# When the zeros of four accumulators are written, and by whose queue: a graph layer with scatters

## The chip, the cores and the metric

The kernel runs on one core of a Trainium2 chip. The metric is the device time of one execution in microseconds (us), median of several runs; less is better. The core has five engines that run side by side, each with its own instruction stream in order: PE (matrix products; PEld is its weight load), DVE and ACT (element work), POOL (here above all the indexed scatters) and SP (here only issues DMAs). DMAs can be issued from SP, ACT and POOL.

## The reference, cut to what matters

```
h = relu(layernorm(x))                              # 6250 nodes x 128
x1 = h @ W_in
W_ij = (ssp(f_ij @ W_f1 + b_f1) @ W_f2 + b_f2) * cutoff    # 200000 edges
out = segment_sum(x1[dst] * W_ij, src, 6250)
return x + ssp(out @ W_o1 + b_o1) @ W_o2 + b_o2     # ssp(v) = softplus(v) - log 2
```

Here dst, by which x1 is gathered, is sorted; src, by which the sum is made, is random.

## The kernel before, in words

**Quads.** The edges are cut into 391 quads of 512 edges. A software pipeline (line 944) takes one quad an iteration: in iteration i, z of quad i+1 (feature matmul, `s1_pe`), softplus of quad i (`s1_exp`, `s1_ln` on ACT, `s1_guard` on DVE), gather and second matmul of quad i-1 (`s2_pe_x`, `s2_pe_w`), their product (`s2_m`), the sum of equal rows of quad i-2 inside chunks of 128 edges (`s3_pe`), its copy for quad i-3 (`s3_copy`, line 377, ACT) and the scatter of quad i-4 (`s3_scatter`). A copy goes to a staging tile `s`, of which there are five: the copy of a quad waits until the scatters of the quad five plain quads before it have landed.

**Plain and sorted quads.** From quad 8 on, two of five quads are "sorted": they are permuted by node group and added in SBUF (`accT`), and only their overflow is scattered. Quads 0 to 7 are all plain, with four scatters each; then 9, 11, 12, 14, 16 and so on are.

**Scatters.** A scatter adds 128 rows to one of four accumulators in memory (`acc0` to `acc3`, 6400 rows of 128 floats). It is an indirect DMA with addition issued by POOL, and it waits until the previous scatter into the same accumulator has landed. `acc_of` gives scatter k its accumulator: 0 below `K1_END` = 2, k % 2 below `K2_END` = 8, k % 3 below 140, then k % 4.

**Zeros.** Each accumulator must be zero before its first scatter. `zero_piece` writes a tenth, 320 KB, from a zeroed tile. POOL issues accumulator 0's ten pieces. SP issues accumulator 1's ahead of the loop (line 773), behind the loads of quads 0 to 3 (`load_sc(0)`, `load_sc(1)`) and a feature block (`fb_load(1)`). Lists `Z2` and `Z3` tell at which iteration SP issues each piece of accumulators 2 and 3: 0, 0, 1, 1, 2, 2, 3, 3, 4, 4 and 5, 7, ..., 23. Within an iteration such a hook comes after the loads of that iteration.

**Loads.** `load_sc(s)` loads features (`ft`), source indices (`sb`), relative rows (`rb`) and table rows (`wn`) of quads 2s and 2s+1, and is called at iteration 2s-4; its tiles have three buffers. `half_load(k)`, at iterations 1 and 2, loads the index rows of the second half of the edges, which DVE turns into relative rows in `half_piece` (line 723) two or more iterations later.

**Order.** The order of instructions on each engine follows the order of the calls (`manual_schedule`). In the built program each DMA issued from SP or ACT takes one of eight completion counters in turn, and waits before it is issued until the DMA eight places earlier, from either engine, has landed.

Of the kernel before, what the change touches and what calls it, by code (L numbers as in the profile page):

```python
# [46 lines left out]
def tile_gnn(ctx: ExitStack, tc: tile.TileContext, x, fB, cT, srcT, srcr, dstr, win_, wf1, wf2, bias, bo1c, wo1,  # L47
             wo2, consts, ident, out, n_edges):
    nc = tc.nc
# [17 lines left out]
    ACC_R = NP + P  # L67
    GN = NP // GRP
    ZR = 10 if ACC_R % 10 == 0 else 1
    K1_END, K2_END, K3_END = 2, 8, 140  # L70
    Z2, Z3 = [0,0,1,1,2,2,3,3,4,4], [5+2*j for j in range(10)]
    CE = min(128, EP // P)
    mpq = sorted_quads(NQ)
    mpi = {q: n for n, q in enumerate(mpq)}
# [68 lines left out]
    def zero_piece(eng, k, j, parts=1):  # L143
        v = accs[k].rearrange("(p t) f -> p (t f)", p=P).rearrange("p (r e) -> r p e", r=ZR)
        w = ACC_R // ZR // parts
        for h in range(parts):
            eng.dma_start(v[j][:, h * w:(h + 1) * w], zero[:, :w])
# [66 lines left out]
    def prep_rm(g):  # L214
        T = groups[g][1]
        rm = wk.tile([P, 4, P], F32, tag="rm", name="rm", bufs=1)
        nc.vector.tensor_tensor(rm[:, :T], pst[g]["xs"][:, :T], pst[g]["x3"][:, :T, 0], op=ALU.subtract)
        pst[g]["rm"] = rm

    def prep_x2(g):  # L220
        T = groups[g][1]
        nc.scalar.copy(pst[g]["x3"][:, :T, 1], pst[g]["rm"][:, :T])

    def prep_x3(g):
        o, T = groups[g]
        w = T * P
        x3 = pst[g]["x3"]
        nc.vector.tensor_tensor(x3[:, :T, 2], pst[g]["rm"][:, :T], x3[:, :T, 1], op=ALU.subtract)
        tab_write(g)

    def tab_write(g):
        o, T = groups[g]
        nc.sync.dma_start(tab[o * 3:(o + T * P) * 3, :].rearrange("(t p k) f -> p t k f", t=T, k=3),
                          pst[g]["x3"][:, :T])
        del pst[g]

    def fb_load(b):
        t_ = ld.tile([P, FE], F32, tag="fb", name="fb", bufs=2)
        nc.sync.dma_start(t_, fB[b].rearrange("r e -> (r e)").rearrange("(p e) -> p e", p=P))
        fst[b] = {"f": t_}  # L240
# [424 lines left out]
    def src_cast(s, lo, hi, eng, tag, **kw):  # L665
        s16 = wk.tile([HALF, hi - lo], I16, tag=tag, name="s16", **kw)
        eng.tensor_copy(s16, idx[s, lo][1])
        nc.sync.dma_start(src16[s * HALF:(s + 1) * HALF, lo:hi], s16)

    with tc.manual_schedule():  # L670
# [77 lines left out]
        prep_x1(0)  # L748
        prep_rm(0)
        prep_x2(0)  # L750
        prep_x3(0)
        src_cast(0, 0, SC, nc.gpsimd, "pt")
        ws = cp.tile([K1, P], BF16, name="ws")
# [16 lines left out]
            load_sc(1)  # L770
        if NB > 1:
            fb_load(1)
        for j in range(ZR):
            zero_piece(nc.sync, 1, j)

        hooks = {}

        def at(i, point, fn, *a):
# [524 lines left out]
```

## Time and profile before

| | us |
|---|---|
| runs of the kernel before: median (lowest to highest) | 2117.85 (2117.82 to 2121.36) |
| the profiled execution | 2119.3 |
| its span | 2117.0 |
| POOL busy in the span, x1073 | 1695.6 |
| PE, DVE, ACT busy | 1915.6, 1763.7, 1789.3 |

The page shares busy time by engine, cuts the span into 40 slices of 53 us, and follows the chain that ended last. Its first slices differ from the later ones:

```
PE   3778999999999999998989999999999999998946
DMA  7987767777777777777777777777777777777639
GB/s 265 242 183 132 149 129 146 141 157 144 149 141 147 133 151 145 141 145 142 148 133 157 139 136 152 143 146 152 136 146 139 129 152 137 139 154 144 111 38 241
```

A digit is the busy share of a slice in tenths. In the first three slices PE is not yet full and the DMA engines move more than later. The other views used below are the timeline (start, length, engine, line, operation, and in brackets the engine's idle time before it with what ended it), the chain of waits (start, length, what), and windows (length, busy time of PE, PEld, DVE, ACT and POOL with counts, granted clock of PE, DMA share, GB/s).

### The profile page before, as it was taken

Reading aid. Unit: us, or ns where it says so; the run is one execution under the profiler, and the core shown is the slowest. Engines: PE = TensorE matmul, PEld = TensorE weight load, DVE = VectorE, ACT = ScalarE, POOL = GpSimd, SP = SyncE. Lnnn points to the kernel's source line nnn. Section 1 sums busy time; section 2 is a strip of 40 time slices with the busy share of each in tenths; the row PEclk is TensorE's granted clock in tenths of the full one; section 3 lists DMA queues with packets and bytes.
Section 4 is the critical chain, followed back from the end, with each engine's and each line's share of the span. In section 5 each row is a group of like instructions: output and inputs, shape, how many; then the busy total and the mean of one; then the engine's idle time right before and its main releaser. Section 6 shows DMA issues by size and latency. Waiting matters only on the chain.

```text
span 2117.0 us, 56533 instructions
## 1 busy us (share of the span) xinstructions
PE 1915.6 (90%) x19769; PEld 1392.3 (66%) x19769; DVE 1763.7 (83%) x4710; ACT 1789.3 (85%) x4781; POOL 1695.6 (80%) x1073
## 2 busy tenths in 40 slices
PE   3778999999999999998989999999999999998946
PEld 2556667676666667666767677777767666766724
DVE  4768888888989898888898989889888878897825
ACT  4688889998988899898989999999899898988804
POOL 2678888888888888888888888888888888887874
PEclk9899999999999999999999999999999999999977
DMA  7987767777777777777777777777777777777639
GB/s 265 242 183 132 149 129 146 141 157 144 149 141 147 133 151 145 141 145 142 148 133 157 139 136 152 143 146 152 136 146 139 129 152 137 139 154 144 111 38 241
DMA packets 395696, 315.17 MB, mean 149 GB/s; under 512 B 94959, under 2 KB 335130, under 8 KB 395410
## 3 DMA queue, kind: packets, MB, share of 16 engines
q1 hardware_dynamic: 245858, 240.57, 38.9%
q0 software_dynamic: 149264, 70.91, 35.3%
q8 instruction: 155, 2.54, 0.5%
q14 instruction: 131, 1.07, 0.2%
q10 hardware_dynamic: 288, 0.07, 0.0%
HBM read 173.32 MB, written 138.06 MB: 147 GB/s over the span
## 4 chain that ended last, share of the span: by engine, by line
PE 32%; ACT 20%; DVE 19%; DMA 10%; POOL 10%; issue 7%; SPq 2%; ACTq 0%; DVEq 0%; POOLq 0%
POOL acc L417 10%; DMA acc<-s,ji 8%; PE un L620 8%; PE W L347 7%; PE pq L527 6%; ACT xc L352 5%; PE pp L369 4%; ACT mst L533 3%; DVE so L605 3%; ACT e L295 3%; ACT e L294 2%; ACT e L300 2%; DVE pm L503 2%; ACT s L377 2%; DVE a L324 1%
## 5 line engine op out<-in xcount | busy, mean ns | idle before, releaser
L417 POOL DMA_INDIRECT acc<-s,ji x955 | 1538.3, 1611 | 350.3 <-issue 222.8
L527 PE MATMUL pq<-pt,pm 128*128 128x387 bf16 x2432 | 484.1, 339 | 26.5 <-ACT s L377 19.2
L352 ACT ACTIVATE xc<-xg,cb 128x128 f32<-128x128 f32 x1564 | 446.4, 374 | 46.9 <-PE xg L339 45.0
L347 PE MATMUL W<-w,a 128*128 128x128 f32 x3128 | 461.7, 292 | 0.0
L347 PEld LDWEIGHTS W<-w,a 128*128 128x128 f32 x3128 | 386.2, 194 | 41.8 <-issue 2.3
L620 PE MATMUL un<-so,mst 32*128 32x392 bf16 x7296 | 355.1, 331 | 41.8 <-DVE pr L467 18.4
L527 PEld LDWEIGHTS <-pm 128*128 128x128 bf16 x2432 | 238.6, 99 | 187.7 <-issue 36.1
L620 PEld LDWEIGHTS <-mst 32*128 32x128 bf16 x7296 | 223.0, 94 | 169.3 <-issue 63.0
L324 DVE SCALAR_TENSOR_TENSOR a<-z,e 128x512 f32<-128x512 f32 x391 | 267.2, 683 | 70.2 <-ACT e L300 70.0
L300 ACT ACTIVATE e<-e,con 128x512 f32<-128x512 f32 x391 | 282.3, 722 | 12.7
L369 PEld LDWEIGHTS pp<-m,eq 128*128 128x128 f32 x1912 | 255.0, 195 | 37.2 <-DVE accT L631 23.6
L369 PE MATMUL pp<-m,eq 128*128 128x129 f32 x1912 | 261.4, 280 | 17.0 <-DVE accT L631 15.0
L533 ACT CAST mst<-pq 128x387 bf16<-128x387 f32 x608 | 260.4, 480 | 8.3 <-PE pq L527 8.3
L377 ACT COPY s<-pp 128x258 f32<-128x258 f32 x478 | 167.1, 391 | 116.2 <-PE pp L369 64.8
L295 ACT ACTIVATE e<-e 128x512 f32<-128x512 f32 x391 | 246.5, 630 | 12.4
L294 ACT ACTIVATE e<-z 128x512 f32<-128x512 f32 x391 | 242.0, 619 | 16.7 <-PE z L289 16.1
L357 DVE TENSOR_TENSOR m<-W,xc 128x512 f32<-128x512 f32 x239 | 164.0, 686 | 80.4 <-ACT xc L352 75.4
L517 DVE TENSOR_TENSOR pt<-pt 128x512 f32<-128x512 f32 x304 | 209.9, 691 | 0.0
L503 DVE TENSOR_SCALAR pm<-iot,pos 128x576 bf16<-128x576 f16 x608 | 197.5, 387 | 0.0
L631 DVE TENSOR_TENSOR accT<-un,accT 128x392 f32<-128x392 f32 x288 | 142.5, 556 | 47.3 <-PE un L620 32.1
L357 DVE TENSOR_TENSOR pt<-W,xc 128x512 f32<-128x512 f32 x152 | 104.5, 688 | 82.1 <-ACT xc L352 80.7
L289 PE MATMUL z<-ft,ws 123*128 123x512 bf16 x391 | 151.9, 389 | 17.9 <-DMA ft<-fsd 17.9
(156 smaller groups left out, 2693.2 us busy)
## 6 DMA issues: line engine op xcount, KB each, us to landing
sb<-src SPq DMA_DIRECT2D x195, 256.0 KB
ft<-fsd SPq DMA_DIRECT2D x195, 240.0 KB
rb<-reld SPq DMA_DIRECT2D x391, 64.0 KB
fsd<-f SPq DMA_DIRECT2D x49, 480.0 KB
fb<-in_fB_dram SPq DMA_DIRECT2D x49, 320.0 KB
fsd<-f SPq DMA_DIRECT2D x49, 320.0 KB
acc<-s,ji POOLq DMA_INDIRECT x955
wn<-tab SPq DMA_DIRECT2D x782, 15.8 KB
```

The source lines that it names most:

```text
L294: nc.scalar.activation(e, st[q]["z"], AF.Abs)
L295: nc.scalar.activation(e, e, AF.Exp, scale=-1.0)
L300: nc.scalar.activation(e, e, AF.Ln, bias=half, scale=0.5)
L324: nc.vector.scalar_tensor_tensor(a, st[q]["z"], 0.0, st[q]["l"], op0=ALU.max, op1=ALU.add)
L347: nc.tensor.matmul(W[:, c, :], st[q]["a"][:, c * P:(c + 1) * P], w2, start=False, stop=(c == 3))
L352: nc.scalar.mul(xc[:, c, :], st[q]["xg"][:, c, :], late["c", q // CQ][:, 4 * (q % CQ) + c:4 * (q % CQ) + c + 1])
L357: nc.vector.tensor_tensor(m[:, :, :P], st[q]["W"], st[q]["xc"], op=ALU.mult)
L369: nc.tensor.matmul(pp[:, c, :129], st[q]["eq"][:, k, :], m[:, k, :129], start=True, stop=True)
L417: nc.gpsimd.indirect_dma_start(out=accs[k][:, :], out_offset=bass.IndirectOffsetOnAxis(ap=ji, axis=0), in_=s, in_offset=None, compute_op=A ...
L527: nc.tensor.matmul(t[:, :PW], mp[q]["pm"][:, c, s * P:(s + 1) * P], high(mp[q]["pt"][:, c:c + 1, :PW])[:, 0], start=(c == 0), stop=(c == 3))
L533: nc.scalar.copy(mp[q]["ms", s][:, :PW], mp[q].pop(("q", s))[:, :PW])
L620: nc.tensor.matmul(ts[g][:, :GN], mp[q]["ms", s][v, k * P:(k + 1) * P], mp[q]["oh"][v], start=(q == qs[0] and k == 0), stop=(q == qs[-1] a ...
```

## The change

Accumulator 1's zeros are issued from ACT, after the second part of the table is made (`prep_x2(0)`) and ahead of ACT's first work on a quad. The pieces of accumulator 2 are issued at iterations 2 to 8, those of accumulator 3 at 11 to 20, one in each. Accumulator 2 takes part from scatter 20 on instead of 8.

```diff
-    K1_END, K2_END, K3_END = 2, 8, 140
-    Z2, Z3 = [0,0,1,1,2,2,3,3,4,4], [5+2*j for j in range(10)]
+    K1_END, K2_END, K3_END = 2, 20, 140
+    Z2, Z3 = [2, 3, 4, 5, 6, 6, 7, 7, 8, 8], [11 + j for j in range(10)]
...
         prep_x2(0)
+        for j in range(ZR):
+            zero_piece(nc.scalar, 1, j)
         prep_x3(0)
...
             fb_load(1)
-        for j in range(ZR):
-            zero_piece(nc.sync, 1, j)
-
         hooks = {}
```

In the built program SP's and ACT's own order stays as it was apart from these pieces. Scatters 8 to 19 go to accumulators 0 and 1 in turn; all others go where they went.

## The prediction

> **What bounds it now.** I read the page first. Its chain is shared among all engines, and its costliest row is the scatter:
>
> ```profile
> PE 32%; ACT 20%; DVE 19%; DMA 10%; POOL 10%; issue 7%; SPq 2%; ACTq 0%; DVEq 0%; POOLq 0%
> L417 POOL DMA_INDIRECT acc<-s,ji x955 | 1538.3, 1611 | 350.3 <-issue 222.8
> ```
>
> No single engine is the bound. The change touches only iterations 0 to 23, and scatter k lands in the same accumulator as before from k = 20 on. So the question is how much earlier or later the loop leaves its first 120 us; after that everything is carried along one for one. Windows of 140 us show that: PE is busy 79.0 of the first 135 us and 124 to 135 of each later 140.
>
> Then the timeline of 20 to 60 us, for SP's queue and for who waits on it:
>
> ```profile
> 22.96 0.60 ACT L294 ACTIVATE e<-z 128x512 f32<-128x512 f32 x1 [5.91 <-PE z L289]
> 32.62 7.77 SPq L147 DMA_DIRECT2D acc<-accT  x10
> 40.43 0.75 SPq L270 DMA_DIRECT2D ft<-fsd  x1
> 45.57 0.61 PE L289 MATMUL z<-ft,ws 123*128 123x512 bf16 x1 [6.59 <-DMA ft<-fsd]
> 51.36 0.23 DVE L723 TENSOR_SCALAR base_i<-half,con 98x2 int32<-98x2 int32 x1 [8.83 <-DMA half<-in_dstr_dram]
> ```
>
> SP spends 7.77 us on the ten zero pieces of accumulator 1; the feature load of quads 4 and 5 is queued behind them, and PE idles 6.6 us for it. Next DVE idles 8.8 us for a half-index load that stands behind that load and two pieces of accumulator 2.
>
> Last, the chain of waits from 85 to 125 us and POOL's timeline. In the chain "issue" before ACT L377 is a wait for the scatter issued at 108.02 (scatter 23): the copy of quad 12 reuses the staging tile of quad 5.
>
> ```profile
> 91.06 6.63 DMA acc<-s,ji
> 97.96 6.10 DMA acc<-s,ji
> ...
> 108.55 6.54 issue
> 115.08 0.04 ACTq L377
> 115.12 0.04 issue
> 115.16 0.65 ACT s L377 x2
> ```
>
> ```profile
> 49.23 1.65 POOL L417 DMA_INDIRECT acc<-s,ji  x1 [23.90 <-ACT ji L398]
> 56.30 1.65 POOL L417 DMA_INDIRECT acc<-s,ji  x1 [5.42 <-DMA acc<-s,ji]
> 62.34 1.54 POOL L417 DMA_INDIRECT acc<-s,ji  x1 [4.38 <-DMA acc<-s,ji]
> ...
> 68.05 1.53 POOL L417 DMA_INDIRECT acc<-s,ji  x1 [2.33 <-DMA acc<-s,ji]
> ...
> 72.72 1.62 POOL L417 DMA_INDIRECT acc<-s,ji  x1 [1.30 <-DMA acc<-s,ji]
> ...
> 76.58 1.54 POOL L417 DMA_INDIRECT acc<-s,ji  x1 [0.30 <-issue]
> ...
> 101.65 1.63 POOL L417 DMA_INDIRECT acc<-s,ji  x1 [0.30 <-ACT e L295]
> ```
>
> These are scatters 0, 1, 2, 4, 6, 8 and 20. A scatter costs POOL 1.54 + 0.30 = 1.84 us, but the next one into the same accumulator waits for its landing. So the early loop is two races: loads against PE and DVE up to 60 us, the stream of scatters from there to 115 us. The change helps the first and holds the second back.
>
> **1. Ten pieces move from SP to ACT.** SP loses 7.77 us ahead of the load of quads 4 and 5. ACT gains ten issues after L222 ends at 17.05, and they are not ten times the 0.45 us of its two constant loads: in the built program each DMA of SP or ACT waits for the one eight places before it (which is why SP's pieces went out 0.8 us apart after the third). ACT's seventh piece waits for the first quad's ft (used by PE at 22.34), the ninth for rb (used by DVE at 24.66), the tenth for the seventh piece. With the four pieces already in flight delaying these by about 1 us, and about 3 us for the seventh piece to land, the tenth leaves near 27 (estimate). Behind it waits ACT's first exponential, at 22.96 before: +4.5 us. Part of this is hidden: quad 0 waited for wn until 26.73 anyway, and quad 2 for its own load until 31.5. I take z of quad 2 at 33, +1.5. Bounds: 0 if ACT is free at 23; +4.5 if nothing hides it.
>
> The Trainium skill (DMA: Bandwidth & Descriptors, Issuing engines are not separate DMA queues) speaks against a gain: DMAs of all issuers run on the same 16 engines, and a second issuer only saves issue time. Rows of the windows view (DMA share and GB/s last):
>
> ```profile
> 16.00:18.00 2.00, 0.00 (x0) 0.00 (x0) 1.47 (x5) 0.40 (x1) 0.00 (x0) 1.00 0.32 97
> 18.00:20.00 2.00, 0.00 (x0) 0.00 (x0) 1.82 (x8) 0.00 (x0) 0.00 (x0) 1.00 0.70 210
> 36.00:42.00 6.00, 2.95 (x17) 1.87 (x16) 3.20 (x5) 5.33 (x15) 0.00 (x0) 0.93 1.04 411
> ```
>
> By the rule alone the 3.28 MB of zeros delay the load of quads 4 and 5 as much as before: no gain. By the rows they now start where the engines are 30 to 70% idle (16 to 24 us: about 3 us of idle capacity) and not at 36 to 42, where they are full. I take the rows: ft of quads 4 and 5 is issued near 34 instead of 40.4, and z of quad 4 moves from 45.6 to about 42: **-3 us**, bounds 0 (the rule) and -6 (all of PE's stop). Scatter 0 (49.23) follows quad 4's exponentials, so it also starts 3 us earlier. DVE's half-index work gains more, 5 to 7 us, but scatters, not DVE, come last later.
>
> **2. Pieces of accumulators 2 and 3 later.** Eight pieces leave 46 to 60 us, two stay there. Scatters 0 and 1, which both go to accumulator 0, returned after 7.07 and 6.04 us under them (49.23, 56.30, 62.34). Without them I take 5.5 each: -2.1 us. The pieces reappear at iterations 4 to 8, about eight of them where five stood, so no lower return is assumed there. Accumulator 2 is complete near 85 us, well ahead of scatter 20. Accumulator 3 enters at scatter 140 in both: no cost.
>
> **3. Third accumulator at scatter 20 instead of 8.** Twelve scatters alternate between two. From the rows, 8 to 20 took 101.65 - 76.58 = 25.1 us with three. With two, each pair costs one return: 5.71 and 4.67 in the rows of scatters 2, 4 and 6, in a lighter stretch; 6.6 and 6.1 plus 0.3 in the chain of 91 to 104 us, with three in flight. I take 5.5; bounds 4.67 and 6.9. Five returns and two issues: 5 x 5.5 + 2 x 1.84 = 31.2, **+6.1 us** (bounds +2.0 and +13.1). Scatter 8 itself now waits for scatter 6: 2 to 8 becomes 5.71 + 4.67 + 5.5 = 15.9 instead of 14.2: +1.6.
>
> **Sum.** Scatter 8: -3 - 2.1 + 1.6 = -3.5 us. Scatter 20: -3.5 + 6.1 = +2.6. Scatters 20 to 23 and the landing at 115.0 keep their 13.4 us, so ACT's copy moves from 115.2 to 117.8; three pieces that lay at 138 to 156, where POOL leads again, are gone: about -0.5. Total **+2 us**. The profiled execution took 2119.3 (span 2117.0), so 2121.3 for it; it was 1.4 above the median of the runs, so 2120 for the median.
>
> **Rivals.**
> *The gain stays*: with two scatters in flight they return in about 4.4 us (below 4.67, since fewer transfers compete), pair cost 25.7 for part 3, so +0.6 there and +0.5 for scatter 8, and the load stage gives 5: 2112. For it: the shortest returns of the trace are those with two accumulators. Against: DMA share is 0.86 to 1.08 from 78 to 114 us.
> *The stream decides, on the slow side*: pairs return in 6.4 us as the chain of 91 to 104 us has them, +10.6 in part 3, +2.5 at scatter 8, -5 before: +8, 2126. It decides from a return of about 5.9. For it: exactly these waits are the chain now. Against: with two in flight, and PE held back, fewer loads compete.
> *ACT does not get out ahead*: the pieces wait on the first loads and the first loads on them, ACT is late by the full 4.5 us, quad 4 gains nothing: +5, 2123.
>
> **Numbers.** No change can be told within 0.2%, 4.2 us. Forecast 0.44 (2115 to 2122); gain stays 0.21; stream slow 0.27; ACT blocked 0.08. Faster 0.21, same 0.44, slower 0.35. The forecast's own range is 2115 to 2122; the range asked for takes in both bounds of the return and the start, 2112 to 2129.
>
> **What would show it.** Part 1: ACT's first L294 near 27 with L147 on ACT's queue ahead of it; z of quad 4 near 42, PE's 6.6 us stop gone; DVE's L723 near 45. Part 2: returns of scatters 0 and 1 near 5.5. Part 3: scatters 8 to 19 in pairs 5.5 apart, POOL idle for "DMA acc<-s,ji" between 14 and 130 us up from 18.9; ACT L377 of quad 12 near 118 with a longer idle ahead. I am wrong if pairs return in under 4.7 or over 5.9 us, or if the copies of quads 9 to 12 don't wait for scatters.

## The result, and the profile after

The changed kernel takes 2127.49 us (median of 7 runs, 2122.78 to 2130.72); the kernel before took 2117.82 in the same 7 rounds (2113.17 to 2121.36). The ratio is 1.0047, 95% interval 1.0031 to 1.0063: 9.7 us slower, some 7 to 13. The time lies inside the range of the prediction. The forecast case "no change that can be told" did not come; the nearest rival was the slow stream of scatters at 2126. The profiled execution took 2127.5 (span 2125.2), 8.2 more than the one of before.

The page's costliest group hardly moves, since only the first 24 of 391 iterations differ; the shares of the chain shift by up to 5 points against those before (PE 32%, ACT 20%, POOL 10%), which is not read further here:

```profile
PE 37%; ACT 25%; DVE 16%; DMA 9%; issue 7%; POOL 5%; SPq 1%; ACTq 0%; DVEq 0%; POOLq 0%
L417 POOL DMA_INDIRECT acc<-s,ji x955 | 1536.1, 1608 | 359.8 <-issue 215.9
```

The loss is in the first 125 us. Timeline of ACT, PE, SP and DVE after, 15 to 50 us:

```profile
16.63 17.40 ACTq L147 DMA_DIRECT2D acc<-accT  x10
34.13 0.60 ACT L294 ACTIVATE e<-z 128x512 f32<-128x512 f32 x1 [17.16 <-DMA acc<-accT]
...
26.47 1.01 PE L289 MATMUL z<-ft,ws 123*128 123x512 bf16 x2 [13.45 <-DMA ft<-fsd]
35.01 0.58 PE L339 MATMUL xg<-wn,oh 63*128 63x128 bf16 x4 [6.99 <-DMA wn<-tab]
38.79 0.63 PE L289 MATMUL z<-ft,ws 123*128 123x512 bf16 x1
...
46.20 0.38 PE L289 MATMUL z<-ft,ws 123*128 123x512 bf16 x1
...
34.21 0.34 SPq L270 DMA_DIRECT2D ft<-fsd  x1
...
39.84 0.42 SPq L270 DMA_DIRECT2D ft<-fsd  x1
...
49.90 0.22 DVE L723 TENSOR_SCALAR base_i<-half,con 98x2 int32<-98x2 int32 x1
```

The same places before:

```profile
22.34 1.01 PE L289 MATMUL z<-ft,ws 123*128 123x512 bf16 x2 [9.32 <-DMA ft<-fsd]
25.46 1.26 SPq L270 DMA_DIRECT2D ft<-fsd  x1
26.73 0.80 PE L339 MATMUL xg<-wn,oh 63*128 63x128 bf16 x4 [2.84 <-DMA wn<-tab]
31.50 0.58 PE L289 MATMUL z<-ft,ws 123*128 123x512 bf16 x1 [1.98 <-DMA ft<-fsd]
```

ACT stands at its ten zero pieces from 16.6 to 34.0 us, and its first exponential comes 11.2 us later than before (22.96). PE's stop of 6.6 us ahead of quad 4 is gone, but 8.3 us more now lie ahead of quad 0: 13.45 us for its features instead of 9.32, and 6.99 for its table rows instead of 2.84. Quad 2 is 7.3 us late (38.79 against 31.50), quad 4 0.6 (46.20 against 45.57). SP issues the load of quads 2 and 3 8.8 us later than before (34.21 against 25.46), and so that of quads 4 and 5 at 39.84, hardly earlier than the 40.43 of before.

The windows after (DMA share and GB/s last) show where the zeros went:

```profile
18.00:20.00 2.00, 0.00 (x0) 0.00 (x0) 1.83 (x8) 0.00 (x0) 0.00 (x0) 1.00 1.01 377
24.00:30.00 6.00, 1.54 (x3) 0.24 (x3) 0.00 (x0) 0.00 (x0) 1.26 (x3) 1.00 1.02 403
36.00:42.00 6.00, 5.08 (x23) 4.20 (x24) 4.88 (x7) 4.96 (x11) 0.00 (x0) 1.00 0.65 190
```

The engines are now full at 18 to 20 us (0.70 before) and at 24 to 30 (0.98 before), and have room at 36 to 42 us (1.04 before).

Then the stream of scatters, in POOL's timeline after (scatters 0, 1, 2, 8 and 20):

```profile
51.76 1.65 POOL L417 DMA_INDIRECT acc<-s,ji  x1 [26.50 <-ACT ji L398]
57.88 1.57 POOL L417 DMA_INDIRECT acc<-s,ji  x1 [4.47 <-DMA acc<-s,ji]
61.45 1.54 POOL L417 DMA_INDIRECT acc<-s,ji  x1 [2.00 <-DMA acc<-s,ji]
...
79.09 1.54 POOL L417 DMA_INDIRECT acc<-s,ji  x1 [1.81 <-DMA acc<-s,ji]
...
111.30 1.54 POOL L417 DMA_INDIRECT acc<-s,ji  x1 [0.31 <-ACT e L294]
```

The steps, against 49.23, 62.34, 76.58 and 101.65 before: start +2.5; scatters 0 to 2 take 9.7 us instead of 13.1 (-3.4); 2 to 8 take 17.6 instead of 14.2 (+3.4); 8 to 20 take 32.2 instead of 25.1 (+7.1). Together +9.6, and scatter 20 is at +9.65. Between 14 and 130 us POOL waits 28.8 us for landings of scatters, 18.9 before. The chain of waits after hands this on to ACT:

```profile
17.93 6.48 DMA src<-s
...
75.74 6.91 DMA acc<-s,ji
...
82.91 5.82 DMA acc<-s,ji
...
89.00 6.03 DMA acc<-s,ji
...
95.29 5.21 DMA acc<-s,ji
...
109.26 8.53 DMA acc<-s,ji
...
123.97 0.65 ACT s L377 x2
```

From 75 to 100 us it goes from landing to landing in accumulator 1 (scatters 7, 9, 11 and 13); at 123.97 ACT copies quad 12, 8.8 us later than before (115.16), after idle stops of 4.8, 7.4, 2.0, 5.3 and 3.6 us at its copies of this stretch. By their first product on PE (z), quads 16 to 20 are 8.7 to 8.8 us late, and that stays, with some wandering (4.8 to 12.4 from quad 30 on, 7.5 at the last), to the end.

### The profile page after: what moved, and what is told of

It reads as the page before. It is cut to its first block, busy times and chain, and to the rows that moved or that the text cites. A ratio compares the mean times of both kernels' runs of the same rounds, so it can differ in the third digit from the quotient of the medians.

```text
span 2125.2 us, 56530 instructions
## 1 busy us (share of the span) xinstructions
PE 1914.4 (90%) x19769; PEld 1392.6 (66%) x19769; DVE 1762.2 (83%) x4710; ACT 1787.9 (84%) x4781; POOL 1695.4 (80%) x1073
## 4 chain that ended last, share of the span: by engine, by line
PE 37%; ACT 25%; DVE 16%; DMA 9%; issue 7%; POOL 5%; SPq 1%; ACTq 0%; DVEq 0%; POOLq 0%
PE un L620 11%; PE W L347 8%; DMA acc<-s,ji 7%; PE pq L527 7%; ACT xc L352 6%; POOL acc L417 5%; ACT mst L533 4%; PE pp L369 4%; ACT e L295 4%; ACT e L294 3%; ACT e L300 3%; DVE so L605 3%; ACT s L377 2%; DVE pm L503 2%; PE z L289 1%
## 5 line engine op out<-in xcount | busy, mean ns | idle before, releaser
L295 ACT ACTIVATE e<-e 128x512 f32<-128x512 f32 x391 | 246.5, 630 | 12.4
L339 PE MATMUL xg<-wn,oh 63*128 63x128 bf16 x1564 | 156.4, 221 | 13.2 <-DMA wn<-tab 7.0
```

Of the source, the lines that this page charges most:

```text
L295: nc.scalar.activation(e, e, AF.Exp, scale=-1.0)
```

## The experiments

Theory A: most of the loss is the stretch in which scatters alternate between two accumulators. Theory B: it is ACT's stop at its zeros. All times are medians, compared with runs of the kernel before on the same chip. Two places of each trace carry the reading: scatter 20, and ACT's copy of quad 12. A single trace's total is no guide: in their later parts the profiled executions drift by several us against each other. The ratio is an estimate of its own with its interval; it can differ from the quotient of the two medians by 0.0008.

| | edit | scatters 8 to 20 (us) | copy of quad 12 at | median, before | ratio (95%) |
|---|---|---|---|---|---|
| before | | 25.1 | 115.2 | | |
| changed | all | 32.2 | 124.0 | 2127.5, 2117.8 | 1.0047 (1.0031 to 1.0063) |
| e1 | K2_END = 20 alone | 34.4 | 122.7 | 2125.5, 2118.7 | 1.0039 (1.0023 to 1.0055) |
| e2 | zeros on ACT alone | 27.6 | 117.7 | 2119.8, 2118.7 | 1.0008 (0.9998 to 1.0018) |
| e3 | changed, zeros back on SP | 32.8 | 120.6 | 2121.9, 2118.7 | 1.0022 (1.0011 to 1.0032) |
| e4 | changed, ACT's zeros as one DMA | 30.0 | 121.9 | 2126.6, 2118.7 | 1.0043 (1.0024 to 1.0061) |
| d1 | K2_END = 32 alone | 36.3 | 127.8 | 2129.2, 2117.3 | 1.0054 (1.0038 to 1.0070) |
| n1 | K1_END = 0 | 25.1 | 114.4 | 2117.9, 2117.3 | 1.0005 (0.9996 to 1.0015) |
| n2 | K1_END = 0, K2_END = 12 | 28.8 | 114.6 | 2118.0, 2117.3 | 1.0006 (0.9994 to 1.0018) |
| n3 | n2 with later lists | 33.1 | 115.8 | 2116.1, 2117.3 | 0.9986 (0.9974 to 0.9999) |
| e6 | changed, K1_END = 0 | 36.1 | 119.9 | 2126.6, 2119.1 | 1.0029 (1.0015 to 1.0043) |
| n4 | acc1's zeros at iteration 1 | 28.7 | 113.7 | 2116.5, 2119.1 | 0.9985 (0.9969 to 1.0000) |
| n5 | acc1's zeros on POOL | 29.7 | 117.9 | 2117.3, 2119.1 | 0.9993 (0.9981 to 1.0005) |

**e1, K2_END alone.**

```diff
-    K1_END, K2_END, K3_END = 2, 8, 140
+    K1_END, K2_END, K3_END = 2, 20, 140
```

> Only K2_END goes from 8 to 20; zeros stay where they were. Theory A (the two-accumulator stretch is most of the loss): scatter 0 stays at 49.2 us, scatters 8 to 20 take 31 to 32 us instead of 25.1, ACT's copy of quad 12 moves from 115 to 122 or more, time +6 to +8 us against the kernel before. Theory B (ACT's stop at the zeros is the loss, the stretch is hidden): time within 2 us of before, the copy of quad 12 at 115 to 117.

Theory A. Scatter 0 is at 48.6, scatters 8 to 20 take 34.4 us (more than the 31 to 32 expected), and ACT's copy of quad 12 is 7.5 us later. In its timeline, scatters 8 and 20 and the copy:

```profile
78.72 1.54 POOL L417 DMA_INDIRECT acc<-s,ji  x1 [3.23 <-DMA acc<-s,ji]
...
113.17 1.54 POOL L417 DMA_INDIRECT acc<-s,ji  x1 [0.30 <-ACT e L300]
...
122.68 0.65 ACT L377 COPY s<-pp 128x258 f32<-128x258 f32 x2 [5.11 <-issue]
```

**e2, ACT alone.**

```diff
         prep_x2(0)
+        for j in range(ZR):
+            zero_piece(nc.scalar, 1, j)
...
-        for j in range(ZR):
-            zero_piece(nc.sync, 1, j)
```

> Only accumulator 1's zeros move from SP to ACT. Both theories: ACT stands at its zeros until 33 or 34 us and z of quad 2 is near 39. Theory A: the load of quads 4 and 5 makes up most of it, scatter 0 at 50 to 53 us, scatters 8 to 20 in about 25 us, time +1 to +4 us. Theory B: scatter 0 and all behind it are late by what ACT lost, time +8 to +10 us.

ACT starts at 34.1 as in the changed kernel, quad 2 is 7.3 us late and scatter 0 3.7 us. Scatters 2 to 15 are within 1.1 us of before: the late start is absorbed. A delay comes back later (scatter 20 3.5 us, quad 16 2.5 us), and scatters 8 to 20 take 27.6 us instead of about 25. The time is +1.1 us with an interval that takes in none. Theory B, with +8 to +10 us, falls.

**e3, the changed kernel without ACT's part.**

```diff
-        for j in range(ZR):
-            zero_piece(nc.scalar, 1, j)
...
+        for j in range(ZR):
+            zero_piece(nc.sync, 1, j)
```

> The changed kernel with accumulator 1's zeros back on SP, behind the loads of quads 0 to 3. Theory A: scatter 0 near 48 us, scatters 8 to 20 in about 32 us, time +4 to +7 us against before (that is 3 to 5 less than the changed kernel). Theory B: -2 to +1 us against before.

The median is 3.2 us over before, between the two expectations and nearer to A; the ratio, 1.0022, makes it 4.7, inside A. The new lists of zeros do help: scatters 1 to 4 are 3.2 to 5.0 us earlier than before. Then the stretch costs its 7.7 us (32.8 instead of 25.1), and scatter 20 is 7.2 late. Set against the changed kernel (1.0047), ACT's part seems to cost more here than alone (1.0008): with the stream behind at most landings, less absorbs its late start. The intervals of e3 and the changed kernel just touch, so this is likely, not shown.

**e4, one DMA on ACT.**

```diff
-        for j in range(ZR):
-            zero_piece(nc.scalar, 1, j)
+        nc.scalar.dma_start(accs[1].rearrange("(p t) f -> p (t f)", p=P).rearrange("p (r e) -> p r e", r=ZR),
+                            zero.unsqueeze(1).to_broadcast([P, ZR, ACC_R // ZR]))
```

> The changed kernel with the ten pieces on ACT as one DMA of 3.28 MB, which takes one completion counter instead of ten. If the counters hold ACT (each piece waits for a DMA eight places earlier): ACT's first exponential at 23 to 27 us instead of 34.1; the second table load of quad 0 then waits for the whole DMA, so quad 0's product is near 31; scatter 0 at 46 to 50; time 1 to 5 us less than the changed kernel, still over before because of the stretch. If bandwidth holds ACT (an issue lasts until the engines take its bytes): ACT's first exponential at 30 us or later, and the time of the changed kernel.

Neither clause as written. ACT's issue no longer holds it, but its first exponential comes at 29.7, because PE's first product waits for features until 29.12. Timeline of PE in e4:

```profile
29.12 1.01 PE L289 MATMUL z<-ft,ws 123*128 123x512 bf16 x2 [16.08 <-DMA ft<-fsd]
```

and the chain of waits in e4:

```profile
17.96 9.50 DMA src<-s
```

against before:

```profile
18.01 2.56 DMA src<-s
```

That small write of indices, without which SP can't read them back, took 2.56 us before, 6.48 in the changed kernel with five pieces issued around it, and 9.50 here with all of them in front. Quad 2 is at 39.8, as late as with ten pieces (38.8). So freeing ACT gives nothing back: zeros in flight during the first loads delay the loads themselves. SP's own issues are slower too (the four of quads 0 and 1's table rows take 4.9 us in the changed kernel and 2.9 here, 2.2 before); how much of that comes from the counters that it shares with ACT was not separated.

**d1, the stretch twice as long.** K2_END = 32 in the kernel before.

> The kernel before with K2_END = 32: the two-accumulator stretch is twice as long as with 20. If the stream of scatters sets the early loop: scatters 8 to 32 take about 24 x 2.7 = 65 us, some 14 more than before at scatter 32, and the time is +12 to +16 us against before, twice that of K2_END = 20. If the loss of K2_END = 20 was a one-off (one collision of a scatter with loads): +6 to +8 as with 20.

The median is 11.9 us over before, just under what was expected. But the trace tells it otherwise than expected: scatter 20 is 14.1 us late and scatter 32 13.7, so the second half of the stretch lost nothing more against before. There fewer scatters come (from quad 8 on only three of five quads scatter in full), and two accumulators keep pace. They win nothing back either: in e1, which has three from scatter 20 on, the delay goes from 11.5 us at scatter 20 to 7.8 at scatter 32. That fits a median 5 us above that of e1, but the intervals overlap and each has one trace: not shown. ACT's stop at quad 12's copy:

```profile
127.75 0.65 ACT L377 COPY s<-pp 128x258 f32<-128x258 f32 x2 [8.01 <-DMA acc<-s,ji]
```

The stretch from 8 to 20 is the same in e1 and d1 and took 34.4 and 36.3 us: about 2 us is chance.

**n1 and n2, an earlier stream in the kernel before.** K1_END = 0, then also K2_END = 12.

> The kernel before with K1_END = 0, so that scatters 0, 1, 2 alternate between accumulators 0 and 1 and not all wait on accumulator 0. If the stream sets the early loop: scatter 2 at 56 to 57 us instead of 62.3, but scatter 8 can't start before accumulator 2 is zero at about 75.8 us, so scatter 20 gains 0 to 3 us and the time -3 to 0. If it does not: time unchanged within 1 us.

> The kernel before with K1_END = 0 and K2_END = 12. If the stream sets the early loop: scatter 2 about 6 us earlier, scatters 8 to 12 cost about 2 us more than with three accumulators but don't wait for zeros; ACT's copies of quads 9 to 12 wait 2 to 5 us less, time -2 to -5 us against before. Otherwise within 1 us of it.

Scatters 2 to 6 are 5 to 7 us earlier in both; scatter 16 is at 92.6 and 92.4 against 92.9 and the time is unchanged. In n1 the lead goes in one step: scatter 8 stands 5.5 us and leaves at 76.7, as before (76.6), which is where the expectation had put the end of accumulator 2's zeros; the profile names no releaser. In n2 it goes from scatter 8 to 13, which take 13.8 us instead of 10.7, with waits for landings ahead of 8, 10 and 11. Scatter 16, the first of quad 4, leaves right behind its predecessor in both, as it did before, so it did not wait for its indices in either. An early stream thus met the next limit within about 30 us, but both limits belong to the stream itself, its zeros and its landings; a lead with the zeros ready and three accumulators from scatter 8 on was not tried.

**e6, the same edit in the changed kernel.**

> The changed kernel with K1_END = 0: scatters 0 to 2 alternate between accumulators 0 and 1. In the kernel before, the same edit made scatters 1 to 6 five to six us earlier and the time no shorter, since scatter 16 then waited for its indices. If the changed kernel's loss is a stream that is late from scatter 8 on with nothing to wait for but landings, a start that is 3 to 6 us earlier is kept to scatter 23: ACT's copy of quad 12 at 118 to 121 us instead of 124.0, time 3 to 6 us less than the changed kernel. If the loss lies elsewhere (ACT's stop, or a later stage): the time of the changed kernel, +8 to +10 against before.

ACT's copy of quad 12 comes at 119.9, 4.1 us earlier than in the changed kernel:

```profile
119.92 0.65 ACT L377 COPY s<-pp 128x258 f32<-128x258 f32 x2 [5.21 <-DMA acc<-s,ji]
```

Scatter 8 is 4.6 us earlier than in the changed kernel, as expected of a stream that is the bound. But scatter 20, the other place, is only 0.7 us earlier (110.6 against 111.3), since scatters 8 to 20 take 36.1 us here. The ratio, 1.0029 against 1.0047, points to a gain, but the intervals overlap: one of the two places bears the expectation out, the time does not settle it.

**n3, n4, n5, towards a better version.** All have K2_END = 12, accumulator 2's pieces at 2, 2, 3, 3, 4, 4, 5, 5, 6, 6 and accumulator 3's at 11 to 20. n3 and n5 have K1_END = 0, n4 has 2. Accumulator 1's pieces: in n3 on SP as before, in n4 on SP behind the first half-index load, in n5 on POOL behind accumulator 0's. The edits of n4 (in the loop of `half_load`) and n5:

```diff
+            for j in range(5 * k, 5 * k + 5):
+                at(1 if spread else 0, "L", zero_piece, nc.sync, 1, j)
...
+        for j in range(ZR):
+            zero_piece(nc.gpsimd, 1, j)
```

> Accumulator 1's zeros on SP as before, K1_END = 0, K2_END = 12, accumulator 2's pieces at iterations 2 to 6 in pairs, accumulator 3's at 11 to 20. If later zeros let the first scatters return sooner (as the changed kernel without ACT's part showed: scatters 1 to 4 were 3 to 5 us earlier) and the stream is the bound: scatter 12 some 5 us earlier than before, time -3 to -7 us. If pipeline stages other than the stream take over at about 100 us: -1 to +1.

> Accumulator 1's zeros stay on SP, but behind the loads of quads 4 and 5 and the first half-index load (iteration 1); K2_END = 12, lists as in n3_lists. If PE's stop of 6.6 us and DVE's of 8.8 us at 40 to 51 us are on the path that ends last: z of quad 4 at 40 to 41 us, scatter 0 at 44 to 46, DVE's half-index work at 44 to 46, time -3 to -8 us against before. If later waits absorb them, as they absorbed the earlier scatters: -2 to +1.

> Accumulator 1's zeros on POOL, behind accumulator 0's, where POOL is idle from 25 to 49 us; K1_END = 0, K2_END = 12, lists as in n3_lists. If zeros that are in flight from 22 to 35 us delay the first loads as ACT's did: z of quad 2 at 35 to 38 us and no gain at quad 4. If only an issuer that stands hurts: z of quad 2 at 32 to 33, z of quad 4 at 40 to 41, time -3 to -6 us against before.

n3 is 1.2 us faster by the medians (ratio 0.9986, 0.2 to 5.5 us by the interval), less than hoped: it is 6.7 us ahead at scatter 8 and 1.3 behind at scatter 20. n4 does what the change seemed to offer: quad 4 is at 38.7 (6.8 us earlier), quad 6 at 53.6 (7.8 earlier), but quad 8 at 70.8, 0.5 earlier. Its chain of waits in between starts with a load of source indices, issued right behind the ten pieces, that takes 6.60 us, and goes on in SP's queue. Its ratio is 0.9985 with an upper end at 1.0000. n5 shows quad 2 at 33.7, 2.2 us late against 7.3 with ACT's zeros, and quad 4 at 46.9, 1.3 late against 0.6: zeros issued by an idle engine, which takes none of the counters of SP and ACT, delay the loads too. n3 is the only version whose interval lies below both kernels, and so narrowly that, among as many comparisons as these, it may be chance.

## Why the prediction was right or wrong

**The range and the third part held.** The stretch of two accumulators was put at 31.2 us, +6.1; it took 32.2, +7.1 (30.0 to 36.3 in the other five runs with it), and its pairs of scatters returned in about 5.7 us ((32.2 - 3.7) / 5), where I had 5.5. e1 shows that it makes a loss of this order alone. The time lies in the range because the bounds of this part were wide; the start came outside its own bounds, so that the range held is in part luck.

**The step that failed is "I take the rows".** The Trainium skill's rule (DMA: Bandwidth & Descriptors, Issuing engines are not separate DMA queues) said that DMAs of all issuers run on the same engines, and by it quad 4 gained nothing. I set it aside because the engines were 30 to 70% idle from 16 to 24 us, and put the start at -3 us. It was +2.5, outside my bounds of 0 to -6: quad 4 came at +0.6, near what the rule gave, and ACT then had a backlog (in the chain of waits it works without a gap from 42.97 to 51.49). I counted about 3 us of idle capacity and did not set the zeros against it: 3.28 MB at the 411 GB/s of my own row take 8.0 us (estimate). The rest, some 5 us, had to come out of the loads of quads 0 to 3, which I had let slip by 1 us. These loads form a chain (write indices, read them back, then rows of the table), each short and each waited for, and zeros in front lengthened it (2.56 to 6.48 us for the first link). So the load of quads 4 and 5 left at 39.84 and not near 34. The bound of 0 was wrong too: I had left out that a delay in the first loads can exceed what SP gains. DVE's half-index work gained 1.5 us (49.90 for 51.36), not 5 to 7.

**ACT's stop was under-sized**: to 34 us, not 27. The mechanism was right: the sixth and seventh pieces left at 24.43 and 26.36, as the index write (24.41) and the features (PE's product at 26.47) landed. But I let the loads that it waits for slip by 1 us; features came 4.1 us later (26.47 against 22.34) and the pieces behind them in turn. Its cost in time was small alone (e2), and e4, where ACT's issue no longer held it, gave nothing back. How much of the changed kernel's time the late loads cost is open: the intervals of e3 and the changed kernel just touch.

**Part 2** was put at -2.1 us and came out at -3.4, but that is no proof of it. With the lists alone (e3) scatters 0 to 2 take 10.6 us instead of 13.1, which bears it out; with the old lists and a late start (e2) they take 10.2. So part of the 3.4 is the late start absorbed.

**Scatters 2 to 8** were put at +1.6 and took +3.4. I saw that about eight pieces would lie there where five had stood, and allowed them nothing; but they are hardly the cause of the other 1.8 us: with the old lists this stretch takes 16.2 and 17.5 us (e1, d1), with the new ones 16.8 to 17.6 (the changed kernel, e3, e4, e6). The cause stays open.

**The sum** was +2 where +8.2 was measured in the trace. As book-keeping, the start is 5.5 us of the difference, part 3 1.0, scatters 2 to 8 1.8, less 1.3 in part 2; that makes 7.0 at scatter 20 and the rest is inside what the later part of a trace drifts. It is not a list of causes, since e2 shows that a late start need not last. The mechanism of the slow rival (pairs decide, from a return of 5.9) was right in kind, not in its number: pairs returned in about 5.7 us, below that point. The chance for slower, 0.35, was too low.

## What to carry to other kernels

When bulk writes are moved to another queue, follow the loads that are in flight beside them, not only the queue that is freed, and set the bytes against the idle share: what does not fit delays the loads around it, and in a chain of short loads that are each waited for it lengthens every wait that it lies in front of. Serial scatters into one target cost a landing each, so the number of targets in turn sets the pace wherever the scatters are behind; count in landings. Before adding up gains and losses, look for the next wait that would absorb them: here a start 3.7 us late was down to 0.7 us two scatters on (e2), and leads of 5 to 7 us were gone within about 30 us (n1, n2).

## What was not expected

Zero pieces issued by ACT from 16.6 us on made a small DMA of SP's, issued 1.3 us later on another queue, land 3.9 us later (6.48 instead of 2.56), and one large DMA made it 9.50, 6.9 later. The large one's 3.28 MB take 8.0 us at 411 GB/s, 6.7 of them still ahead when the small one is issued (estimate): being small and on a queue of its own did not bring it ahead of the bulk. The 49 runs of the kernel before beside e1 to e4 span 2109.7 to 2126.5 us, 0.8%, where the first three spanned 0.17%; differences of 0.2% needed a dozen runs or more of each.
